# Two softmax additions ahead of a step's values and logits, and bank reads emitted with the last matmul

## The chip, the cores and the metric

The kernel runs on one core of a Trainium2 chip. The metric is the device time of one execution in microseconds (us). Three runs of the kernel before took 3520.87, 3521.09 and 3527.97 us; the median is 3521.09. Engines are named as in the profile: PE is TensorE (its weight loads are PEld), DVE is VectorE, ACT is ScalarE, POOL is GpSimd, SP is SyncE, which issues the DMAs.

## What is computed

Eight images of 512 channels and 32 x 32 pixels go through two layers, in float32. The reference, cut to what matters (`cbs` is a convolution, a batch norm and a SiLU; `_gn` is a group norm of 32 groups; `mask` lets only pairs of channels of one group through, `p` is a permutation):

```python
def bot_attention(x, qkv_w, rw, rh):          # x: 256 channels, 4 heads of 64
    q, k, v = conv2d(x, qkv_w, 0) ...
    logits = einsum('bhdi,bhdj->bhij', q, k + (rw + rh)) * 64 ** -0.5
    a = softmax(logits, axis=-1)              # 1024 x 1024 per head
    return einsum('bhij,bhdj->bhdi', a, v)

t = cbs(x, cv1_w, cv1_bn, 0)                  # on _gn(x)
ys = [t[:, :256], t[:, 256:]]
for i in range(2):
    z = cbs(ys[-1], m_cv1_w[i], m_cv1_bn[i], 1)           # 3x3
    z = bot_attention(z, m_qkv_w[i], m_rw[i], m_rh[i])
    z = silu(bn_eval(conv2d(z, m_cv2_w[i], 0), m_cv2_bn[i]))
    ys.append(ys[-1] + z)
x = x + cbs(concatenate(ys), cv2_w, cv2_bn, 0)            # layer 0
x = x + (1x1 conv of _gn(x) with conv * t_gain * mask * s_gain)[:, p[p]]   # layer 1
```

## The kernel before

**Softmax units.** The attention of one image and block is cut into four units: two pairs of heads (`hp`) by two halves of 512 query columns. With 8 images and 2 blocks these are 64 units. The logits are made transposed: 128 keys stand on the partitions, 512 queries in the free dimension, one PSUM bank for each head of the pair. A unit has eight pieces `t` of 128 keys (`KT`). `logits(t)` makes two banks `lg` on PE (L435), ACT copies each to an SBUF tile `st` (L441), and DVE takes the running maximum `mx` from the bank (L446, from t = 1 on). `top` transposes the maxima on PE (`mt`, L454) and reduces them on DVE (`nm`, L455); `spread` transposes them back, over all partitions, into the PSUM tile `mb` (L462). `soften(t)` adds `mb`, which holds the negated maximum, to `st` on DVE (L466), takes the exponential on ACT in place (L467) and adds up on POOL (`sum`, L472). `values(t)` multiplies with v on PE into the one bank `po` (L478). `finish` sums over the partitions on PE (`den`, L490), copies on ACT (`rb`, L492); `divide` takes the reciprocal and multiplies on DVE, in halves (L497, L499).

**Steps.** The main loop runs over 16 slots (image, block) of four units. A unit's four steps take t = 0, 2, 4, 6. A step treats two pieces of the unit `u`, two pieces of logits of the next unit `nxt`, and then a share of background work (`advance`). The maxima of `nxt` and the additions of `u` are tied in the order in which they are emitted (`in_turn`): on DVE none passes another. What else stands between them is set by the Tile scheduler, which orders each engine's instructions by when its own model has them ready.

**Background work.** `filler` goes through a slot's list (`slot_filler`): the 3x3 convolution of the next slot (`conv3`, by a transform in six products `m`), its projections (`project`: `qk`, `v`), the second 1x1 convolution of the slot before (`conv_m2`), and from a queue (`Background.take`) the first convolution of later images (`First`), the concatenated convolution (`Second`: `cv2`) and the second layer (`Last`: `l1`). Each is a generator that emits matmuls and yields a price in us; `advance` takes from it until the share of the step is reached. `accumulate` (L166 to L174) emits the matmuls of one sum into one bank and yields 1.72 after each two of them, the last time after the last matmul; only when it is resumed does the caller emit the reader of the bank (for instance `bn_silu`, L130 on ACT) and what follows it. `conv3` and `project` yield in the same way between the last matmul of a product and its readers. After product 4 these readers are six DVE operations, L288 to L293.

**Buffers.** One pool of five PSUM banks (`ps_f`) serves logits, `mt`, `den` and all background sums; `mb` has two banks and `po` one of their own. Which bank a new tile gets follows from the order in which the tiles before are released in the scheduler's model. The `st` tiles have ten buffers.

Of the kernel before, what the change touches and what calls it, by code (L numbers as in the profile page):

```python
# [22 lines left out]
P = 128  # L23
NB = 8
CT = 4
# [14 lines left out]
def conv_preact_kernel(ctx: ExitStack, tc: tile.TileContext, x, cv1, cv2, mcv1, qkv, mcv2, bn, rw, rh, conv, s_in, t_in, out):  # L40
# [92 lines left out]
    class GroupNorm:  # L133
# [30 lines left out]
        def apply(self, k, dst, src):  # L164
            nc.scalar.activation(dst, src, AF.Identity, bias=self.off[:, k : k + 1], scale=self.rstd[:, k : k + 1])  # L165


    def accumulate(ps, terms):

        for n, (w, moving) in enumerate(terms):  # L170
            nc.tensor.matmul(ps, w, moving, start=(n == 0), stop=(n == len(terms) - 1))  # L171
            if n % 2 and n < len(terms) - 1:
                yield 1.72
        yield 1.72 if len(terms) % 2 == 0 else 0.86  # L174

    class Image:
        def __init__(self, n):
# [23 lines left out]
        def conv1(self, h, tiles, order=(1, 0)):  # L201
            n = self.n
            for cp in order:
                w = weights(f"w_cv1_{n}_{h}_{cp}", (CT, 256), cv1[cp])
                for co in range(IT):
                    ps = bank(f"cv1_{n}_{cp}_{co}_{h}")
                    yield from accumulate(ps, [(w[:, k, ts(co, P)], tiles[k // 2][:, k % 2]) for k in range(CT)])
                    t = half_tile(f"y0_{n}_{cp}_{co}_{h}")
                    bn_silu(t, ps, BN_CV1 + IT * cp + co)
                    load(y_dram[n][cp][:, co, ts(h, HALF)], t)  # L210

        def load_y(self):
            assert self.halves == 2
# [4 lines left out]
        def conv3(self, i):  # L218
# [15 lines left out]
            def product(r, u):  # L234
                w = weights(f"w_m1_{name}_{r}", (IT, IT, 3, P), w_m1[i][r])
                ps = bank(f"m1_{name}_{r}")
                terms = [(c, dx) for c in range(IT) for dx in range(3)]
                for co in range(IT):
                    for j, (c, dx) in enumerate(terms):
                        nc.tensor.matmul(  # L240
                            ps[:, ts(co, 256)].rearrange("p (t x) -> p t x", x=F),
                            w[:, co, c, dx],
                            u[:, 9 * c : 9 * c + 8, dx : dx + F],
                            start=(j == 0),
                            stop=(j == len(terms) - 1),
                        )
                        if j % 3 == 2 and (co, j) != (1, 5):
                            yield 1.33
                yield 1.33
                self.ps = ps  # L250

            z = self.z = qp.tile([P, IT, HW], F32, tag="z", bufs=1, name=f"z_{name}")
# [20 lines left out]
            stt(inner(u4), b, -2.0, a, ALU.mult, ALU.add)  # L273
            yield from product(1, u1)
            nc.scalar.copy(mm[:, 0], self.ps)
            yield from product(2, u2)

            u0, u5 = plane(), plane()
# [3 lines left out]
            stt(inner(u5), b, -4.0, inner(u5), ALU.mult, ALU.add)  # L282
            nc.vector.tensor_tensor(ss[:, 0], mm[:, 0], self.ps, ALU.add)
            nc.vector.tensor_tensor(dd[:, 0], mm[:, 0], self.ps, ALU.subtract)
            yield from product(3, u3)
            nc.scalar.copy(mm[:, 1], self.ps)
            yield from product(4, u4)
            nc.vector.tensor_tensor(ss[:, 1], mm[:, 1], self.ps, ALU.add)  # L288
            nc.vector.tensor_tensor(dd[:, 1], mm[:, 1], self.ps, ALU.subtract)
# [1 line left out]
            stt(y[2], tx(ss[:, 1]), 4.0, tx(ss[:, 0]), ALU.mult, ALU.add)  # L291
            nc.vector.tensor_tensor(ss[:, 0], ss[:, 0], ss[:, 1], ALU.add)
            stt(dd[:, 0], dd[:, 1], 8.0, dd[:, 0], ALU.mult, ALU.add)  # L293
            yield from product(0, u0)
            nc.vector.tensor_tensor(y[0], tx(self.ps), tx(ss[:, 0]), ALU.add)
            yield from product(5, u5)
            nc.vector.tensor_tensor(y[3], tx(self.ps), tx(dd[:, 0]), ALU.add)
            for co in range(IT):
                bn_silu(z[:, co], z[:, co], BN_M1 + IT * i + co)


        def project(self, i):
            name = f"{self.n}_{i}"
            z = self.z
            self.q = qp.tile([P, IT, HW], F32, tag="q", name=f"q_{name}")
            self.k, self.v = [], []
            w = weights(f"w_qkv_{name}", (IT, 768), qkv[i])
            for hp in range(IT):
                k = kp_.tile([P, HW], F32, tag="k", name=f"k_{name}_{hp}")
                v = kp_.tile([P, KT, P], F32, tag="v", name=f"v_{name}_{hp}")  # L310
                self.k.append(k)
                self.v.append(v)
                load(k, r_dram[i][:, hp])
                for sel in (1, 0):
                    for h in range(2):
                        ps = bank(f"qk_{name}_{hp}_{sel}_{h}")
                        yield from accumulate(
                            ps, [(w[:, c, ts(IT * sel + hp, P)], z[:, c, ts(h, HALF)]) for c in range(IT)]
                        )
                        if sel == 0:  # L320
                            nc.scalar.mul(self.q[:, hp, ts(h, HALF)], ps, HD**-0.5)
                        else:
                            dst = k[:, ts(h, HALF)]
                            nc.vector.tensor_tensor(dst, ps, dst, ALU.add)
                for j4 in range(2):
                    ps = bank(f"v_{name}_{hp}_{j4}")
                    for j in range(4):
                        for c in range(IT):
                            nc.tensor.matmul(  # L329
                                ps[:, ts(j, P)],  # L330
                                z[:, c, ts(4 * j4 + j, P)],
                                w[:, c, 512 + P * hp : 512 + P * hp + P],
                                start=(c == 0),
                                stop=(c == IT - 1),
                            )
                    yield 1.77
                    nc.scalar.copy(v[:, 4 * j4 : 4 * j4 + 4].rearrange("p j c -> p (j c)"), ps)


        def conv_m2(self, i):  # L340
# [4 lines left out]
            for h in range(2):  # L345
                res = pair(gr, "gr", f"res_{name}_{h}")
                load(res, y_dram[n][1 + i][:, :, ts(h, HALF)])
                for co in range(IT):
                    ps = bank(f"m2_{name}_{co}_{h}")
                    yield from accumulate(ps, [(w[:, c, ts(co, P)], q[:, c, ts(h, HALF)]) for c in range(IT)])  # L350
                    t = half_tile(f"m2s_{name}_{co}_{h}")
                    bn_silu(t, ps, BN_M2 + IT * i + co)
                    dst = y_rows(co, h) if i == 0 else res[:, co]
                    nc.vector.tensor_tensor(dst, res[:, co], t, ALU.add)
                    load(y_dram[n][2 + i][:, co, ts(h, HALF)], dst)


        def load_ys(self, h):
# [7 lines left out]
        def conv2(self, h, ys):  # L366
# [3 lines left out]
            for cp in range(2):  # L370
                res = pair(gr, "gr", f"xr_{n}_{h}_{cp}")
                load(res, x[n, cp, :, :, ts(h, HALF)])
                for c in range(2):
                    co = 2 * cp + c
                    w = weights(f"w_cv2_{n}_{h}_{co}", (2 * CT, P), cv2[co])
                    ps = bank(f"cv2_{n}_{h}_{co}")
                    yield from accumulate(ps, [(w[:, k], ys[k // 2][:, k % 2]) for k in range(2 * CT)])
                    t = half_tile(f"cv2s_{n}_{h}_{co}")
                    bn_silu(t, ps, BN_CV2 + co)
                    nc.vector.tensor_tensor(res[:, c], res[:, c], t, ALU.add)  # L380
                    self.gn1.stats(co, h, res[:, c])
                load(x2_dram[n][:, h, 2 * cp : 2 * cp + 2], res)


        def load_x2(self, h):
# [12 lines left out]
        def last(self, h, xn):  # L398
            n = self.n
            for cp in range(2):  # L400
# [2 lines left out]
                w = weights(f"w_l1_{n}_{h}_{cp}", (CT, 256), w_l1[cp])  # L403
                for c in range(2):
                    ps = bank(f"l1_{n}_{h}_{2 * cp + c}")
                    yield from accumulate(ps, [(w[:, k, ts(c, P)], xn[k // 2][:, k % 2]) for k in range(CT)])
                    nc.vector.tensor_tensor(res[:, c], ps, res[:, c], ALU.add)
                load(out[n, cp, :, :, ts(h, HALF)], res)

    turn = []  # L410

# [329 lines left out]
    class Background:  # L741
# [15 lines left out]

        def take(self, us, force=False, wait=False):

            done = 0.0  # L760
            while done < us:
                if self.cur is None:
                    self.prepare()
                    if self.first == len(self.items):
# [2 lines left out]
                    if "setup" not in it.past or (clock.now < it.ready and not force):  # L767
                        if not wait:
                            return
                        done += 0.5  # L770
                        yield 0.5
                        continue
                    if clock.now < it.ready:
                        clock.flush()
# [3 lines left out]
                it, g = self.cur  # L778
                cost = next(g, None)
                if cost is None:  # L780
                    self.cur = None
                    continue
                done += cost
                yield cost
# [62 lines left out]
    def start_conv(im, tiles):  # L847
        n = im.n
        for cp in (1, 0):
            w = weights(f"w_cv1_{n}_{cp}", (CT, 256), cv1[cp])  # L850
            for h in range(2):
                for co in range(IT):
                    ps = bank(f"cv1_{n}_{cp}_{co}_{h}")
                    yield from accumulate(ps, [(w[:, k, ts(co, P)], tiles[h, k // 2][:, k % 2]) for k in range(CT)])
                    t = half_tile(f"y0_{n}_{cp}_{co}_{h}")
                    bn_silu(t, ps, BN_CV1 + IT * cp + co)
                    load(y_dram[n][cp][:, co, ts(h, HALF)], t)
        im.halves = 2

    first, second = images[:2]  # L860
# [22 lines left out]
    for s in range(len(slots)):  # L883
# [22 lines left out]
        for j in range(4):  # L906
# [9 lines left out]
            if before:  # L916
                before.finish()
                clock.tick(0.9)
            for t in range(0, KT, 2):
                if t:  # L920
                    u.values(t - 2)
                    u.values(t - 1)
                    clock.tick(2.0)
                u.soften(t)
                if before and t == 0:
                    before.divide(1)
                if nxt:
                    nxt.logits(t)
                    nxt.logits(t + 1)
                    clock.tick(2.0)  # L930
                u.soften(t + 1)
                advance((base + 4 + t) / steps)
            u.values(KT - 2)
            u.values(KT - 1)
# [62 lines left out]
```

## Time and profile before

| | |
|---|---|
| median of the three runs | 3521.09 us |
| the profiled execution, its own time | 3534.95 us |
| its span, first to last instruction | 3533.2 us |
| granted TensorE clock over the span | 0.974 |
| additions L466 | 512, 1212 ns each |
| exponentials L467 | 512, 1056 ns each |
| copies of logits L441 | 1024, 595 ns each |
| maxima L446 | 768 + 128, 680 and 677 ns each |
| sums on POOL L472 | 768 + 128, 1341 and 1328 ns each |
| table loads on ACT, before L130 and L467 | 130 and 128, 1283 ns each |

Times of instructions are of the one profiled execution. A wait row names who waited, for whom, the us in total, how often and the longest; the one named is the one that came last. A matmul of 512 columns in float32 stands as two records in the trace, some 0.43 us each at full clock, so that "x8" in a row of logits is four matmuls, of which those of two heads overlap. A timeline row has start, duration, engine, line, operation, output and inputs, a count, and in brackets the idle time of the engine before it and what ended it. The busy time of the matmuls grows when the clock is granted at half, so that a lower clock shows as PEclk and not as idle time.

### The profile page before, as it was taken

The page shows a single profiled execution, that of the slowest core. Times are in us where ns is not written, and L with a number is a line of the kernel's source. Part 1 is how long each engine was busy: PE and PEld are TensorE (multiplying, and loading weights), DVE is VectorE, ACT ScalarE, POOL GpSimd, SP SyncE. Part 2 cuts the span into 40 slices and gives each one's busy share as a digit, 9 for nine tenths or more (in the row PEclk, how much of TensorE's full clock was granted, in tenths as well). Part 3 has the DMA queues.
Part 4 walks back from the last instruction along what each step waited for, and adds up shares of the span by engine and source line. Part 5 has one row for each costly group of instructions (what it writes and reads, how often), then busy time and mean ns, then how long its engine had stood idle before and what let it go on. Part 6 is the DMA issues. An engine that isn't in the chain of part 4 may idle for free.

```text
span 3533.2 us, 33236 instructions
## 1 busy us (share of the span) xinstructions
PE 3306.7 (94%) x11716; PEld 1562.5 (44%) x11716; DVE 2113.4 (60%) x2717; ACT 1801.2 (51%) x2385; POOL 1257.0 (36%) x971
## 2 busy tenths in 40 slices
PE   6999998999999999999999999999999999999988
PEld 2645434343444445354444444354545344353333
DVE  4435555475756665576756665676756665666641
ACT  3045674755555544554555544645456544645631
POOL 2014333343433433343433334344434433334320
PEclk9899999999999999999999999999999999999989
DMA  7552352231223241333323141332323241523345
GB/s 276 204 199 88 98 173 75 90 107 45 102 75 116 66 143 66 103 130 100 109 80 116 60 152 63 131 113 96 101 94 103 68 148 53 165 67 107 114 160 173
DMA packets 142296, 400.35 MB, mean 113 GB/s; under 512 B 13104, under 2 KB 14384, under 8 KB 142128
## 3 DMA queue, kind: packets, MB, share of 16 engines
q1 hardware_dynamic: 141408, 397.99, 33.8%
q8 instruction: 93, 1.52, 0.2%
q14 instruction: 75, 0.61, 0.1%
q10 hardware_dynamic: 720, 0.23, 0.0%
HBM read 318.47 MB, written 79.69 MB: 113 GB/s over the span
## 4 chain that ended last, share of the span: by engine, by line
PE 62%; DVE 15%; ACT 9%; issue 7%; DMA 4%; POOL 3%; SPq 0%; ACTq 0%; POOLq 0%; DVEq 0%
PE cv L171 13%; PE m L240 9%; PE lg L435 9%; PE po L478 9%; PE l L171 5%; PE qk L171 5%; DVE mx L446 4%; DVE st L466 3%; PE v L329 3%; ACT st L467 3%; POOL sum L472 2%; DVE rb L497 2%; ACT st L441 2%; DMA x<-in_x 2%; PE den L490 2%
## 5 line engine op out<-in xcount | busy, mean ns | idle before, releaser
L472 POOL TENSOR_TENSOR sum<-sum,st 128x512 f32<-128x512 f32 x768 | 1009.3, 1341 | 833.4 <-ACT st L467 833.4
L467 ACT ACTIVATE st<-st 128x1024 f32<-128x1024 f32 x512 | 537.0, 1056 | 644.2 <-DVE st L466 636.9
L446 DVE TENSOR_TENSOR mx<-mx,lg 128x512 f32<-128x512 f32 x768 | 482.6, 680 | 499.2 <-ACT st L441 498.8
L441 ACT COPY st<-lg 128x512 f32<-128x512 f32 x1024 | 534.8, 595 | 328.5 <-PE lg L435 250.0
L466 DVE TENSOR_TENSOR st<-st,mb 128x1024 f32<-128x1024 f32 x512 | 609.8, 1212 | 74.2 <-PE mb L462 74.1
L435 PE MATMUL lg<-q,k 64*128 64x512 f32 x2048 | 620.7, 634 | 25.4 <-DVE mx L446 20.2
L478 PE MATMUL po<-st,v 128*64 128x512 f32 x2048 | 547.6, 622 | 61.1 <-ACT st L467 44.4
L240 PE MATMUL m<-plane,w_m 128*128 128x256 f32 x2304 | 540.7, 389 | 18.8 <-DVE mx L446 9.7
L472 POOL TENSOR_TENSOR sum<-st,st 128x512 f32<-128x512 f32 x128 | 167.2, 1328 | 969.0 <-ACT st L467 969.0
L240 PEld LDWEIGHTS m<-plane,w_m 128*128 128x128 f32 x2304 | 433.5, 193 | 152.9 <-issue 42.4
L171 PE MATMUL cv<-y,w_cv 128*128 128x512 f32 x1024 | 470.7, 603 | 9.0 <-DMA y<-y 6.8
L435 PEld LDWEIGHTS lg<-q,k 64*128 64x128 f32 x2048 | 211.9, 189 | 417.7 <-issue 280.4
L171 PEld LDWEIGHTS cv<-y,w_cv 128*128 128x128 f32 x1024 | 185.8, 191 | 257.7 <-issue 235.8
L478 PEld LDWEIGHTS po<-st,v 128*64 128x64 f32 x2048 | 115.6, 137 | 390.9 <-ACT st L467 169.3
L497 DVE RECIPROCAL rb<-rb 128x256 f32<-128x256 f32 x128 | 215.6, 1724 | 92.3 <-ACT rb L492 92.3
L171 PE MATMUL cv<-x,w_cv 128*128 128x512 f32 x512 | 243.3, 623 | 26.4 <-ACT x L165 15.3
L171 PE MATMUL qk<-z,w_qkv 128*128 128x512 f32 x512 | 234.0, 599 | 15.8 <-DVE mx L446 13.1
L171 PE MATMUL l<-x,w_l 128*128 128x512 f32 x512 | 236.2, 608 | 2.4 <-ACT x L165 2.4
L130 ACT ACT_TABLE_LOAD x130 | 166.8, 1283 | 17.7 <-PE m L171 14.5
L455 DVE TENSOR_REDUCE nm<-mt 128x4 f32<-128x512 f32 x128 | 82.3, 682 | 144.3 <-PE mt L454 144.3
L171 PEld LDWEIGHTS cv<-x,w_cv 128*128 128x128 f32 x512 | 97.1, 198 | 158.0 <-issue 113.2
L467 ACT ACT_TABLE_LOAD x128 | 164.2, 1283 | 2.2
(144 smaller groups left out, 2374.8 us busy)
## 6 DMA issues: line engine op xcount, KB each, us to landing
w_m<-w_m SPq DMA_DIRECT2D x96, 768.0 KB, 4.5
w_cv<-in_cv SPq DMA_DIRECT2D x92, 512.0 KB, 3.6
y<-y SPq DMA_DIRECT2D x64, 512.0 KB, 4.8
x<-in_x SPq DMA_DIRECT2D x56, 512.0 KB, 4.8
y<-y SPq DMA_DIRECT2D x64, 256.0 KB, 3.1
k<-r SPq DMA_DIRECT2D x32, 512.0 KB, 3.8
res<-y SPq DMA_DIRECT2D x32, 512.0 KB, 4.4
xr<-in_x SPq DMA_DIRECT2D x32, 512.0 KB, 4.2
```

Of the source, the lines that this page charges most:

```text
L130: nc.scalar.activation(dst, src, AF.Silu, bias=bn_b[:, col : col + 1], scale=bn_s[:, col : col + 1])
L171: nc.tensor.matmul(ps, w, moving, start=(n == 0), stop=(n == len(terms) - 1))
L240: nc.tensor.matmul(ps[:, ts(co, 256)].rearrange("p (t x) -> p t x", x=F), w[:, co, c, dx], u[:, 9 * c : 9 * c + 8, dx : dx + F], start=(j ...
L329: nc.tensor.matmul(ps[:, ts(j, P)], z[:, c, ts(4 * j4 + j, P)], w[:, c, 512 + P * hp : 512 + P * hp + P], start=(c == 0), stop=(c == IT - 1),)
L435: nc.tensor.matmul(lg[h], self.k[r, ts(t, P)], self.q[r, self.hp, ts(self.half, HALF)], start=True, stop=True)
L441: nc.scalar.copy(st[:, h], lg[h])
L446: in_turn(nc.vector.tensor_tensor(self.mx[:, h], so_far[:, h], lg[h], ALU.max))
L466: in_turn(nc.vector.tensor_tensor(st, st, flat(self.mb), ALU.add))
L467: nc.scalar.activation(st, st, AF.Exp)
L472: nc.gpsimd.tensor_tensor(self.acc[:, h], so_far[:, h], self.st[t][:, h], ALU.add)
L478: nc.tensor.matmul(self.po[HD * h : HD * h + HD], self.v[:, t, ts(h, HD)], self.st[t][:, h], start=(t == 0), stop=(t == KT - 1),)
L497: nc.vector.reciprocal(self.rb[:, r], self.rb[:, r])
```

## The change

Three things are changed. First, in a step both `soften(t)` and `soften(t + 1)` are emitted first, then the values of the step before, then the logits of the next unit; before, `soften(t)` stood between values and logits, and `soften(t + 1)` behind the logits. Second, a generator yields its last price after the reader of the bank and not before it; `accumulate` returns this price and the caller yields it. The price after the second half of a v bank is 0.89 and not 1.77. Third, the prices that close a sum are of the type `Whole`, and `take` ends only behind such a price, so that a task from the queue is not left in the middle of a sum when the list goes on to the next task. Where two sums share a store (`conv2`, `last`), the price of the second comes behind the store. The places not shown below change in the same way as those shown.

```diff
+    class Whole(float):
+        pass
     def accumulate(ps, terms):
         for n, (w, moving) in enumerate(terms):
             nc.tensor.matmul(ps, w, moving, start=(n == 0), stop=(n == len(terms) - 1))
             if n % 2 and n < len(terms) - 1:
                 yield 1.72
-        yield 1.72 if len(terms) % 2 == 0 else 0.86
+        return Whole(1.72)
...
-                    yield from accumulate(ps, [(w[:, k, ts(co, P)], tiles[k // 2][:, k % 2]) for k in range(CT)])
+                    us = yield from accumulate(ps, [(w[:, k, ts(co, P)], tiles[k // 2][:, k % 2]) for k in range(CT)])
                     t = half_tile(f"y0_{n}_{cp}_{co}_{h}")
                     bn_silu(t, ps, BN_CV1 + IT * cp + co)
                     load(y_dram[n][cp][:, co, ts(h, HALF)], t)
+                    yield us
...
-                yield 1.33
                 self.ps = ps
...
             yield from product(1, u1)
             nc.scalar.copy(mm[:, 0], self.ps)
+            yield 1.33
             yield from product(2, u2)
...
             yield from product(4, u4)
             nc.vector.tensor_tensor(ss[:, 1], mm[:, 1], self.ps, ALU.add)
             nc.vector.tensor_tensor(dd[:, 1], mm[:, 1], self.ps, ALU.subtract)
...
             nc.vector.tensor_tensor(ss[:, 0], ss[:, 0], ss[:, 1], ALU.add)
             stt(dd[:, 0], dd[:, 1], 8.0, dd[:, 0], ALU.mult, ALU.add)
+            yield 1.33
             yield from product(0, u0)
...
-                    yield 1.77
                     nc.scalar.copy(v[:, 4 * j4 : 4 * j4 + 4].rearrange("p j c -> p (j c)"), ps)
+                    yield 0.89
...
                     self.gn1.stats(co, h, res[:, c])
+                    if c == 0:
+                        yield us
                 load(x2_dram[n][:, h, 2 * cp : 2 * cp + 2], res)
+                yield us
...
         def take(self, us, force=False, wait=False):
-            done = 0.0
-            while done < us:
+            done, cost = 0.0, Whole()
+            while done < us or not isinstance(cost, Whole):
...
                         done += 0.5
-                        yield 0.5
+                        yield Whole(0.5)
                         continue
...
                 if cost is None:
-                    self.cur = None
+                    self.cur, cost = None, Whole()
                     continue
                 done += cost
                 yield cost
...
             for t in range(0, KT, 2):
+                u.soften(t)
+                if before and t == 0:
+                    before.divide(1)
+                u.soften(t + 1)
                 if t:
                     u.values(t - 2)
                     u.values(t - 1)
                     clock.tick(2.0)
-                u.soften(t)
-                if before and t == 0:
-                    before.divide(1)
                 if nxt:
                     nxt.logits(t)
                     nxt.logits(t + 1)
                     clock.tick(2.0)
-                u.soften(t + 1)
                 advance((base + 4 + t) / steps)
```

More of the change, by code (lines that the diff above doesn't have):

```diff
@@ L284, in conv3 @@
             nc.vector.tensor_tensor(dd[:, 0], mm[:, 0], self.ps, ALU.subtract)
+            yield 1.33
             yield from product(3, u3)
             nc.scalar.copy(mm[:, 1], self.ps)
+            yield 1.33
             yield from product(4, u4)
@@ L293, in conv3 @@
             stt(dd[:, 0], dd[:, 1], 8.0, dd[:, 0], ALU.mult, ALU.add)
+            yield 1.33
             yield from product(0, u0)
             nc.vector.tensor_tensor(y[0], tx(self.ps), tx(ss[:, 0]), ALU.add)
+            yield 1.33
             yield from product(5, u5)
@@ L299, in conv3 @@
                 bn_silu(z[:, co], z[:, co], BN_M1 + IT * i + co)
+            yield 1.33
         def project(self, i):
@@ L316, in project @@
                         ps = bank(f"qk_{name}_{hp}_{sel}_{h}")
-                        yield from accumulate(
+                        us = yield from accumulate(
                             ps, [(w[:, c, ts(IT * sel + hp, P)], z[:, c, ts(h, HALF)]) for c in range(IT)]
@@ L349, in conv_m2 @@
                     ps = bank(f"m2_{name}_{co}_{h}")
-                    yield from accumulate(ps, [(w[:, c, ts(co, P)], q[:, c, ts(h, HALF)]) for c in range(IT)])
+                    us = yield from accumulate(ps, [(w[:, c, ts(co, P)], q[:, c, ts(h, HALF)]) for c in range(IT)])
                     t = half_tile(f"m2s_{name}_{co}_{h}")
@@ L376, in conv2 @@
                     ps = bank(f"cv2_{n}_{h}_{co}")
-                    yield from accumulate(ps, [(w[:, k], ys[k // 2][:, k % 2]) for k in range(2 * CT)])
+                    us = yield from accumulate(ps, [(w[:, k], ys[k // 2][:, k % 2]) for k in range(2 * CT)])
                     t = half_tile(f"cv2s_{n}_{h}_{co}")
@@ L381, in conv2 @@
                     self.gn1.stats(co, h, res[:, c])
+                    if c == 0:
+                        yield us
                 load(x2_dram[n][:, h, 2 * cp : 2 * cp + 2], res)
+                yield us
         def load_x2(self, h):
@@ L405, in last @@
                     ps = bank(f"l1_{n}_{h}_{2 * cp + c}")
-                    yield from accumulate(ps, [(w[:, k, ts(c, P)], xn[k // 2][:, k % 2]) for k in range(CT)])
+                    us = yield from accumulate(ps, [(w[:, k, ts(c, P)], xn[k // 2][:, k % 2]) for k in range(CT)])
                     nc.vector.tensor_tensor(res[:, c], ps, res[:, c], ALU.add)
+                    if c == 0:
+                        yield us
                 load(out[n, cp, :, :, ts(h, HALF)], res)
+                yield us
     turn = []
@@ L853, in start_conv @@
                     ps = bank(f"cv1_{n}_{cp}_{co}_{h}")
-                    yield from accumulate(ps, [(w[:, k, ts(co, P)], tiles[h, k // 2][:, k % 2]) for k in range(CT)])
+                    us = yield from accumulate(ps, [(w[:, k, ts(co, P)], tiles[h, k // 2][:, k % 2]) for k in range(CT)])
                     t = half_tile(f"y0_{n}_{cp}_{co}_{h}")
@@ L857, in start_conv @@
                     load(y_dram[n][cp][:, co, ts(h, HALF)], t)
+                    yield us
         im.halves = 2
```

## The prediction

> **What bounds the kernel now.** I read the busy rows and the 40 slices first, then TensorE's waits, the granted clock by stretches, ScalarE's waits, and the timeline around one long wait. The first row says that TensorE works 94% of the span and no other engine more than 60%.
>
> ```profile
> PE 3306.7 (94%) x11716; PEld 1562.5 (44%) x11716; DVE 2113.4 (60%) x2717; ACT 1801.2 (51%) x2385; POOL 1257.0 (36%) x971
> ```
>
> So a gain can only come out of TensorE's idle time and out of its clock. The built order of both programs is, but for a few swaps, the same on TensorE up to the first unit's softmax (255 us) and from the last unit's maxima on (3360 us); what changes lies between. TensorE's waits in that stretch (who, on whom: us in total, times, longest):
>
> ```profile
> PE po L478 <- ACT st L467: 44.4, 44, 2.9
> PE lg L435 <- DVE mx L446: 20.2, 20, 1.9
> PE qk L171 <- DVE mx L446: 13.1, 19, 0.9
> PE po L478 <- DVE q L499: 10.0, 7, 2.5
> PE m L240 <- DVE mx L446: 9.7, 9, 3.2
> PE m L171 <- DVE mx L446: 8.3, 7, 1.9
> PE v L329 <- DVE mx L446: 8.2, 12, 0.9
> PE cv L171 <- DVE mx L446: 7.8, 8, 2.0
> ```
>
> All rows of that answer together make 156 us. Two kinds are most of it: values (po) that wait for an exponential, 44.4 us, and matmuls of any kind that wait for a maximum (mx), that is for a bank that its last reader has not left: 20.2 + 13.1 + 9.7 + 8.3 + 8.2 + 7.8 = 67.3 us. The other 44 us are spread over the division, activations and planes. The clock in the same stretch (us, busy times, then PEclk):
>
> ```profile
> 255.00:3360.00 3105.00, 2949.88 (x10726) 1384.81 (x10728) 1956.42 (x2448) 1693.64 (x2240) 1200.92 (x918) 0.98 0.31 101
> ```
>
> The records behind that 0.98 are stretches of half clock, 106 us in all, so about 53 us of work lost. They lie behind long waits; this is one (DVE, ACT and PE from 1555 us on):
>
> ```profile
> 1563.02 1.75 DVE L293 SCALAR_TENSOR_TENSOR dd<-dd 128x512 f32<-128x512 f32 x1
> 1564.69 1.87 DVE L446 TENSOR_TENSOR mx<-mx,lg 128x512 f32<-128x512 f32 x3
> ...
> 1567.12 0.67 DVE L446 TENSOR_TENSOR mx<-mx,lg 128x512 f32<-128x512 f32 x1
> 1567.72 2.34 DVE L466 TENSOR_TENSOR st<-st,mb 128x1024 f32<-128x1024 f32 x2
> ```
> ```profile
> 1560.07 2.05 ACT L441 COPY st<-lg 128x512 f32<-128x512 f32 x4 [1.17 <-PE lg L435]
> 1568.96 2.19 ACT L467 ACTIVATE st<-st 128x1024 f32<-128x1024 f32 x2 [6.84 <-DVE st L466]
> ```
> ```profile
> 1559.79 1.02 PE L435 MATMUL lg<-q,k 64*128 64x512 f32 x4
> ...
> 1570.07 1.08 PE L478 MATMUL po<-st,v 128*64 128x512 f32 x4 [2.87 <-ACT st L467]
> 1571.08 3.68 PE L435 MATMUL lg<-q,k 64*128 64x512 f32 x8
> ```
>
> The addition for the odd half of a step stands behind the four maxima of that step, these stand behind conv3's vector work (L288 to L293), the exponential behind the addition, and the values of the next step behind the exponential. TensorE waits 2.87 us, and then eight logit records take 3.68 us; elsewhere eight take 1.99. I matched the values' waits with the program by their order: 41 of the 44, 42.8 us, are for an odd half (t = 1, 3, 5, 7).
>
> **The additions moved ahead.** Nothing is added or removed: in each of 256 steps (64 units of four) one addition (1212 ns, L466), one exponential (1056 ns, L467) and two sums on GpSimd (1341 ns each, L472) move from behind the copies and maxima to ahead of them. No DMA moves with them. The values of an odd half no longer depend on the maxima of their own step: the 42.8 us go. I count 38 and leave 5 for units whose first steps come too soon behind the spread. Each exponential's sums start earlier too, and ScalarE's copies wait 74.2 us for sums (57 times), so that this wait can only shrink.
>
> What it may cost: a copy now stands behind two additions and two exponentials instead of one of each, 1.21 us on VectorE and 1.06 us on ScalarE, and behind the copies wait the maxima, and behind these the banks. The cover is ScalarE's idle time ahead of the copies:
>
> ```profile
> ACT st L441 <- PE lg L435: 245.6, 189, 4.1
> ACT st L441 <- POOL sum L472: 74.2, 57, 3.7
> ```
>
> 245.6 us over 256 steps is 0.96 us a step against 1.06. That alone would be thin. But the built order of the changed kernel puts the first addition directly behind the maxima of the step before in 172 of the 189 steps with t = 2, 4, 6, and both in 139, so they run in VectorE's idle time (40% of the span) while TensorE does background work. Bounds: nothing, and 67 x 1.06 us = 71 us if each of the 256 steps less the 189 idle ones pays a whole exponential. I take 10, near the lower end, because in 126 of 192 steps the built order has both exponentials side by side, and a late copy costs TensorE only when the 5.2 us of background sums (median of a step by the built order and 0.86 us a 512-column matmul) are over before the bank is free. A sentence of the Trainium skill speaks against this part: "TensorE: Matmul & The Clock Gate" (Architectural detail) has ScalarE and VectorE as strict FIFO, so a copy that is ready can't pass an exponential that isn't. The trace agrees (6.84 us of idle ScalarE at 1568.96).
>
> **Bank reads with the last matmul.** The generators now emit the readers before they hand back control. Readers, tables and stores stay as many; the stores go to SP's queue no later than before, and TensorE waits for no DMA in this stretch. The maxima waits fall in two kinds: 58 short ones (under 1 us, 36.1 us) and 17 long ones (31.4 us). The short ones are nearly all 0.6 us: the next background sum was given the bank of the step's first logits, 2.6 us behind their start, although the bank of the sum before had been read (a copy of v ends at 1406.99, the next v sum waits until 1410.77 for a maximum). The bank was given by the order of emission, and there the read came late. With it early, the older bank is free first. I take two thirds, 24 us; bounds 0 and 36. The long ones come where conv3's six operations (5.8 us) stand ahead of a unit's addition, so that exponential, copies and maxima all follow; five of 1.9 us are of this kind at the same place of the pattern. In the built order afterwards both additions stand ahead of those six operations in most of the sixteen convolutions, the maxima still behind. I take half, 16 us; bounds -15 (the maxima come later by as much) and 31. ScalarE's table loads fall from 260 to 244, 16 x 1283 ns = 20.5 us, beside TensorE's work: nothing.
>
> **Ends between sums, and the planner's prices.** The same matmuls run; a sum is no longer cut at a change of task, and two sums of v count 0.89 us instead of 1.77 while 16 records take 1.95. So steps with v get some 1 us more work for each and a later step 3.5 us less per projection. By the built order the thinnest step between logits 1 and values 0 grows from 0.2 to 3.6 us of background. I take nothing for it; bounds -10 and +10, the size of the division's waits (po <- q, 10.0).
>
> **The clock.** There are 28 waits of over 1.6 us (58.9 us together), and the half-clock stretches lie behind such waits. If half of them go, half of the 53 us does: 26 us; bounds 0 and 45. The same page of the Trainium skill (HAM oscillation) asks for gaps over about 3.4 us before the clock falls. By that rule waits of 2 to 3 us cost no clock and the sum would be 26 us smaller; the trace differs, as 3.68 against 1.99 us behind a wait of 2.87 shows.
>
> **Sum.** 38 + 24 + 16 + 26 - 10 = 94 us. The profiled execution took 3534.95 us (span 3533.2 and 1.7 around it), so 3441; the median of the runs is 3521.09, 14 us less, so 3427, and I say 3430.
>
> **Rivals.** (A) Only the odd exponentials gain, and the bank waits come back at other places, since five banks serve four logits and one sum as before: 38 us and a fifth of the clock's 53, less 10, about 39: 3482. For it: the long maxima waits are VectorE's own work. Against it: the short ones are an order of emission, which changes.
> (B) Slower: the copies are late by the second exponential. Place: the copy behind two exponentials, once per step. Price: the 71 us above and, as banks are then late by more than 1.6 us, another 40 of half clock, less 38 for the values and the clock behind them (10): 71 + 40 - 48 = +63, 3584. It decides as soon as more than some 45 of the 256 steps pay the exponential. For it: 0.96 against 1.06 us, and the FIFO. Against it: the additions' place in the built order.
> (C) Nothing: the planner's uneven steps and new waits for the row maxima (nm), now behind conv3's six operations in some units (3 or 4 times by the built order), eat it up: 3520. For it: the waits that are not po or mx, 44 us, are untouched.
> (D) Nearly all goes: 42.8 + 60 + 45 + 15 of the others, 163: 3358.
>
> **Chances.** Forecast 0.56, D 0.10, A 0.16, C 0.06, B 0.12. A measurement of this kernel tells 0.2%, 7 us, from no change. Faster 0.56 + 0.10 + 0.16 = 0.82, same 0.06, slower 0.12. The range takes in A and most of D and leaves B, C and the far end of D out: 3350 to 3515.
>
> **What would show it.** Right: po <- ACT st falls from 44 to under 8 us; the short mx waits to a third; PEclk in 255 to 3360 rises to 0.99; TensorE's idle time in that stretch falls from 156 to about 85 us. Wrong: ScalarE's idle time ahead of the copies is now VectorE's (ACT st L467 <- DVE st L466) while matmuls wait for mx more than 67 us (B); or mb <- nm becomes a row of more than 10 us (C).

## The result, and the profile after

| | before | after |
|---|---|---|
| median of four runs in turn | 3524.53 us | 3412.33 us (3409.66 to 3419.54) |
| ratio after to before, 95% interval | | 0.9674 [0.9655, 0.9692] |
| profiled execution, its own time | 3534.95 us | 3419.54 us |
| its span | 3533.2 us | 3417.8 us |
| granted clock over the span | 0.974 | 0.973 |

The change gains 112 us; 94 were forecast. The busy rows of the page of after, engine by engine, are as before: TensorE 94%, nothing else above 61%.

```profile
PE 3223.6 (94%) x11716; PEld 1559.5 (46%) x11716; DVE 2082.3 (61%) x2717; ACT 1759.5 (51%) x2369; POOL 1241.4 (36%) x971
```

TensorE's busy time fell by 83 us (3306.7 before) with the same number of instructions at the same clock. That was in no term of the sum. The costliest groups (busy us, mean ns of one, idle before and what ended most of it) show two rows that became cheaper, logits and values; first of before, then of after:

```profile
L435 PE MATMUL lg<-q,k 64*128 64x512 f32 x2048 | 620.7, 634 | 25.4 <-DVE mx L446 20.2
L478 PE MATMUL po<-st,v 128*64 128x512 f32 x2048 | 547.6, 622 | 61.1 <-ACT st L467 44.4
```
```profile
L453 PE MATMUL lg<-q,k 64*128 64x512 f32 x2048 | 555.1, 624 | 15.5 <-DVE dd L289 7.9
L496 PE MATMUL po<-st,v 128*64 128x512 f32 x2048 | 516.8, 618 | 31.4 <-ACT st L485 21.1
```

The mean of one record hardly moved, the sum did. 2048 logit records of 634 ns would be 1298 us, and the row has 620.7: what overlaps counts once, so the records of after overlap more. TensorE's waits from 255 to 3245 us, that is from the first softmax to just before the last logits, after (who, on whom: us in total, times, longest):

```profile
PE po L496 <- ACT st L485: 21.1, 14, 2.5
PE m L245 <- DVE z L303: 13.7, 6, 4.1
PE m L245 <- DVE mx L464: 12.8, 8, 3.6
PE l L175 <- DVE mx L464: 8.7, 3, 2.9
PE gm_a L146 <- DVE mv_a L144: 8.1, 4, 3.0
PE lg L453 <- DVE dd L289: 7.9, 3, 2.6
...
PE lg L453 <- DVE mx L464: 2.6, 4, 0.6
```

Values wait half as long, logits hardly for maxima any more; new are, among others, rows for `z` and `dd` (the vector work of conv3). The same stretch in one line: PEclk stands at 0.98, as before.

```profile
255.00:3245.00 2990.00, 2860.61 (x10714) 1381.24 (x10713) 1925.36 (x2450) 1649.35 (x2222) 1184.62 (x918) 0.98 0.32 105
```

To split the difference I gave TensorE's time from the first `mb` to the last one to the matmul that ran, from its start to the next start, less the wait ahead of the next, and kept apart half of the time at half clock (us, from the traces):

| kernel | waits | logits | values | all other matmuls | clock | span |
|---|---|---|---|---|---|---|
| before | 157.2 | 579.8 | 503.2 | 1823.0 | 48.6 | 3533.2 |
| after | 129.7 | 521.3 | 477.5 | 1818.2 | 53.9 | 3417.8 |

Waits give 27.5, logits 58.5, values 25.7, the rest 4.8; the clock takes 5.3. So 84 of the 111 us come from logits and values that take less time, though none was removed. The timeline shows how. A group here is a row of logits records on TensorE, or of values, with no other matmul between them; it is cut when another matmul is put inside. Before (start, us, work; wait in brackets):

```profile
1030.96 5.42 PE L171 MATMUL cv<-y,w_cv 128*128 128x512 f32 x12
1036.31 1.08 PE L478 MATMUL po<-st,v 128*64 128x512 f32 x4
1037.32 1.13 PE L435 MATMUL lg<-q,k 64*128 64x512 f32 x4
1038.37 1.08 PE L478 MATMUL po<-st,v 128*64 128x512 f32 x4
1039.38 1.13 PE L435 MATMUL lg<-q,k 64*128 64x512 f32 x4
...
1047.41 1.12 PE L435 MATMUL lg<-q,k 64*128 64x512 f32 x2
1048.46 1.08 PE L478 MATMUL po<-st,v 128*64 128x512 f32 x4
1049.47 1.98 PE L435 MATMUL lg<-q,k 64*128 64x512 f32 x6
```

And after:

```profile
1011.33 1.94 PE L496 MATMUL po<-st,v 128*64 128x512 f32 x8
1013.20 1.99 PE L453 MATMUL lg<-q,k 64*128 64x512 f32 x8
1015.12 5.42 PE L175 MATMUL cv<-y,w_cv 128*128 128x512 f32 x12
```

Eight records of logits together (four matmuls, two heads) take 1.92 us to the next start. Cut into two and six, the two take 1.05 and the six 1.91: six cost as much as eight, for the matmul whose partner of the other head is not beside it runs alone, and alone it takes as long as a pair (four records, 1.06). That cut costs 1.05 + 1.91 - 1.92 = 1.04 us. Cut in four and four it costs 2 x 1.06 - 1.92 = 0.20, and values in two halves 2 x 1.01 - 1.87 = 0.15. The odd exponentials were late before, and so, as the run with a free order on VectorE below bears out, the scheduler put odd values between the logits or behind some of them. Groups of logits in the built order, by records:

| records | 2 | 4 | 6 | 8 | more |
|---|---|---|---|---|---|
| before | 64 | 32 | 53 | 183 | 1 |
| after | 23 | 12 | 8 | 226 | 7 |

At the durations of the timeline rows, logits and values in the built order come to 1106.5 us before and 1033.5 after, 73 less. A wait inside a group cuts it too, on top of its own length: 12 groups of eight before and 5 after, 13.4 and 5.4 us beyond the waits.

"TensorEngine Tiling (Array Packing)" of the Trainium skill (Key Properties) says that tiles of the array run in parallel and that a change of tiling mode drains TensorE. Here logits use 64 rows, values 64 columns and the background all of the array; the 0.15 to 0.20 us of a cut that leaves pairs whole fits a drain, and the 1.04 us of a cut through a pair fits the lost parallel half.

### The profile page after: what moved, and what is told of

It is laid out like the page before. It is cut to its first block, busy times and chain, and to the rows that moved or that the text cites. A ratio compares the mean times of both kernels' runs of the same rounds, so it can differ in the third digit from the quotient of the medians.

```text
span 3417.8 us, 33275 instructions
## 1 busy us (share of the span) xinstructions
PE 3223.6 (94%) x11716; PEld 1559.5 (46%) x11716; DVE 2082.3 (61%) x2717; ACT 1759.5 (51%) x2369; POOL 1241.4 (36%) x971
## 4 chain that ended last, share of the span: by engine, by line
PE 63%; DVE 11%; ACT 6%; issue 6%; DMA 3%; POOL 2%; SPq 0%; POOLq 0%; DVEq 0%; ACTq 0%
PE cv L175 13%; PE po L496 10%; PE lg L453 10%; PE m L245 9%; PE qk L175 6%; PE l L175 5%; PE v L340 3%; DVE st L484 3%; ACT st L485 2%; PE den L508 2%; DVE mx L464 2%; PE mt L472 2%; DVE rb L515 1%; PE m L175 1%; PE mb L480 1%
## 5 line engine op out<-in xcount | busy, mean ns | idle before, releaser
L490 POOL TENSOR_TENSOR sum<-sum,st 128x512 f32<-128x512 f32 x768 | 998.4, 1330 | 710.1 <-ACT st L485 710.1
L245 PE MATMUL m<-plane,w_m 128*128 128x256 f32 x2304 | 543.6, 391 | 33.2 <-DVE z L303 13.7
L453 PE MATMUL lg<-q,k 64*128 64x512 f32 x2048 | 555.1, 624 | 15.5 <-DVE dd L289 7.9
L496 PE MATMUL po<-st,v 128*64 128x512 f32 x2048 | 516.8, 618 | 31.4 <-ACT st L485 21.1
L490 POOL TENSOR_TENSOR sum<-st,st 128x512 f32<-128x512 f32 x128 | 160.3, 1273 | 978.4 <-ACT st L485 802.4
L175 PE MATMUL cv<-y,w_cv 128*128 128x512 f32 x1024 | 463.5, 601 | 5.2 <-DMA y<-y 4.5
L453 PEld LDWEIGHTS lg<-q,k 64*128 64x128 f32 x2048 | 193.6, 187 | 370.1 <-issue 251.8
L496 PEld LDWEIGHTS po<-st,v 128*64 128x64 f32 x2048 | 125.0, 137 | 343.0 <-issue 220.2
L175 PE MATMUL l<-x,w_l 128*128 128x512 f32 x512 | 244.1, 625 | 19.7 <-ACT x L165 9.6
L175 PEld LDWEIGHTS l<-x,w_l 128*128 128x128 f32 x512 | 97.6, 199 | 147.4 <-issue 114.2
```

Source lines behind the costliest of these rows:

```text
L245: nc.tensor.matmul(ps[:, ts(co, 256)].rearrange("p (t x) -> p t x", x=F), w[:, co, c, dx], u[:, 9 * c : 9 * c + 8, dx : dx + F], start=(j ...
L453: nc.tensor.matmul(lg[h], self.k[r, ts(t, P)], self.q[r, self.hp, ts(self.half, HALF)], start=True, stop=True)
L490: nc.gpsimd.tensor_tensor(self.acc[:, h], so_far[:, h], self.st[t][:, h], ALU.add)
L496: nc.tensor.matmul(self.po[HD * h : HD * h + HD], self.v[:, t, ts(h, HD)], self.st[t][:, h], start=(t == 0), stop=(t == KT - 1),)
```

## The experiments

Two theories to start with. WAITS: the gain is that of the prediction, waits and what follows from them. RUNS: most of it is that logits and values stand in whole groups. Ratios are to before, run in turn on the same chip.

**Part one alone.** Before, with only the new step order:

```diff
+                u.soften(t)
+                if before and t == 0:
+                    before.divide(1)
+                u.soften(t + 1)
                 if t:
                     u.values(t - 2)
```

> Part one alone: both additions of a step first, bank reads and prices as before. Two theories. WAITS (the prediction's): the gain comes out of TensorE's waits, 38 us for the odd exponentials less 10, and no more, so 3524 - 28 = about 3495. RUNS (formed from the two traces): a group of four logit matmuls that stand together takes 1.99 us, a single one cut off 1.12 and the other three 1.98; two values together 1.08, four 1.94. By the built order logits and values take 1057 us at these prices against 1106 before, 49 less, and the po <- ACT st waits fall by some 23 us: about 3450.

3472.49 us, 0.9847 [0.9830, 0.9864]: 54 of the 112 us, between the two. The table's columns: waits 151.4, logits 548.1, values 494.7. Waits fall by 6 only, logits and values by 40. The values' wait for exponentials falls to 16.3 us, but 24 groups of logits now have a wait inside (26.4 us beyond it).

**Parts two and three alone.** After, with the old step order (the diff above, taken back).

> Parts two and three alone: bank reads with the last matmul, tasks end between sums, order of a step as before. WAITS: the bank waits' 40 us and a part of the clock, 50 us: about 3475. RUNS: by the built order logits and values take 1097 us against 1106, so 9 us less and what bank waits fall, 10 to 25: about 3500. By both the odd exponentials' waits (44 us) stay.

3488.50, 0.9889 [0.9874, 0.9903]: 39 us. Waits fall by 27 (157.2 to 130.1), the values' stay at 48.2. The two parts alone make 93 us, together 112.

**Part two alone.** The same, and the background may end within a sum again:

```diff
-            while done < us or not isinstance(cost, Whole):
+            while done < us:
```

> Part two alone: bank reads with the last matmul; order of a step and take's end as before. Together with reads_only (3488) it tells what ending between sums is worth under the old order; no_whole against the changed kernel gave 54 us under the new. If a task left in the middle of a sum holds a bank and so makes a logit matmul wait inside its group of four, lg <- mx stays near 19 us here (6.8 in reads_only, 18.7 in no_whole) and the time is about 3488 + 35 = 3520; logits and values by the built order 1112 us against 1097. If the early reads alone are the gain, 3490.

3517.01, 0.9966 [0.9950, 0.9983]: 8 us by the medians, 12 by the ratio; so some 27 to 31 of the 39 come with part three. Two wait rows of this kernel:

```profile
PE po L496 <- ACT st L485: 48.3, 47, 2.9
PE lg L453 <- DVE mx L464: 20.5, 19, 1.9
```

The logits wait for maxima 19 times, as before (20.2, 20 times); with part three it is 6.8 us, 4 times. The short waits for maxima (under 1 us) come to 37.5 us before, 30.0 with part two, 10.3 with parts two and three.

**Parts one and two.** After, with that same line put back.

> The changed kernel with part three taken out: take ends where its budget ends, in the middle of a sum or not. If ending between sums is worth something by itself, slower than 3412: by the built order logits and values take 1044 us against 1033, 11 us more: about 3423. If only the early reads count, 3412.

3465.89, 0.9812 [0.9787, 0.9838]: a miss for both numbers. Without part three 54 us of the 112 are gone (49 by the ratios), and the logits' waits for banks are back:

```profile
PE lg L453 <- DVE mx L464: 18.7, 19, 1.9
```

Its profiled execution was its fastest, 3453.41 us, and shows 35 us of this loss: waits 132.9, logits 543.4, values 487.7. Against after, 3 us of the 35 are waits and 32 are logits and values; 20 groups of eight have a wait inside (5 in after), which costs 21.8 us beyond the waits. That a task left within a sum holds a bank over the next logits follows from the code; shown is that these waits come and go with part three.

**Order tied, in before.** A manual order on PE keeps logits and values as they are emitted:

```diff
-                nc.tensor.matmul(
+                in_turn_pe(nc.tensor.matmul(
```

> The kernel before, with one thing added: logits and values are tied on TensorE in the order in which they are emitted, so that the scheduler can't put a values matmul between the four logits of a step. RUNS: by the built order logits and values take 1033 us against 1106, as in the changed kernel; 73 us less, less what new waits the tie makes for odd exponentials (up to some 40): 3450 to 3490. WAITS: a tie can only add waits; not faster than 3524, rather 10 us slower.

3554.86, 1.0082 [1.0065, 1.0100]. The groups got cheaper (logits 528.4, less 51), but (waits up to 3300 us):

```profile
PE po L484 <- ACT st L473: 97.2, 63, 3.9
PE lg L441 <- DVE mx L452: 31.3, 21, 4.9
```

The values wait over twice as long, and the clock costs 70.8 us and not 48.6. So whole groups gain nothing by themselves: a late exponential is paid either as cut groups or as waits. Whole groups are worth something only when their input is early.

**Order tied, in after.** The same edit on after.

> The changed kernel with the same tie. RUNS: logits and values 1015 us against 1033 by the built order, 18 us less: about 3394. WAITS: 3412 within its spread, or slower by new waits.

3415.26, 0.9682 [0.9665, 0.9699]: no gain. Logits 498.3, 23 less, but the first values of a unit now wait for the division (po <- q 32.8 us, 5.8 in after) that the scheduler had let other logits fill.

**Groups cut on purpose.** After, tied, with each group of logits cut once after its first matmul and the values apart:

```diff
+                    nxt.one(t, 0)
                     u.values(t - 2)
+                    nxt.one(t, 1)
+                    nxt.one(t + 1, 0)
+                    nxt.one(t + 1, 1)
+                    nxt.rest(t)
                     u.values(t - 1)
+                    nxt.rest(t + 1)
```

(`one` is a bank and its matmul, `rest` the copies and maxima.)

> The price of a cut group by itself: after_tied, with the order of a step made one logit matmul, two values, three logit matmuls, two values (t = 2, 4, 6); the same matmuls and no later inputs. By the built order 182 singles and 189 threes, logits and values 1254 us against 1015. RUNS, if the pieces' prices hold: 3415 + 239 = about 3650, with TensorE's idle time no higher than in after_tied (142 us). If a group's length is not a price of its own, 3415.

3526.92, 0.9997 [0.9982, 1.0012], 112 us more than tied after: all of the change's gain is gone, with the same matmuls and their groups cut. Logits take 691.9 us and values 499.8, 194 and 18 more; the expected time was too high mainly because waits fell to 74.0 (from 142.2) and the clock's cost to 29.2 (from 51.0). Its row of logits:

```profile
L461 PE MATMUL lg<-q,k 64*128 64x512 f32 x2048 | 737.1, 632 | 7.4 <-DVE dd L289 2.7
```

**Free order on VectorE, in before.** The tie between maxima and additions is left out:

```diff
-        if turn:
-            tc.add_manual_dep(instruction.ins, turn.pop().ins.name, IN_ORDER, reason="order of the softmax")
         turn.append(instruction)
```

> The kernel before without the tie between maxima and additions: emission as before, and the scheduler alone orders VectorE. It then puts the odd addition ahead of the maxima nearly everywhere. If the cause of both the waits and the cut groups is the odd addition's place behind the maxima, this is as fast as soften_only, about 3472 (logits and values by the built order 1037 us), and po <- ACT st falls under 20 us. If it is the place of the values in the emission, it stays near 3527. It can also be slower, where several additions run ahead and the maxima, and with them the banks, come later.

3453.48, 0.9780 [0.9760, 0.9802]: 75 us, more than part one. It confirms the cause that the prediction named, the odd addition held behind the maxima: with the scheduler free to pull it ahead, the values' wait is 14.8 us (44.4 before) and logits take 542.0.

**Free order, in after.**

> The changed kernel without the tie between maxima and additions. before_free (3453) was faster than soften_only (3472). If the tie itself costs, some 19 us less here too: about 3393. If the emission order already says what the scheduler would do, 3412 (logits and values by the built order 1037 us against 1033).

3415.79, 0.9694 [0.9679, 0.9709], as after: what the tie cost, part one has already taken.

**Tied, with logits first at t = 2.** The wait for the division is filled with the four logits:

```diff
+                if t == 2 and nxt:
+                    for j in range(4):
+                        nxt.one(t + j // 2, j % 2)
+                    u.values(t - 2)
+                    u.values(t - 1)
+                    nxt.rest(t)
+                    nxt.rest(t + 1)
```

> after_tied, with the logits ahead of the values at t = 2 only, where the values wait for the division of the unit before (po <- q, 32.8 us in after_tied against 5.8 in the changed kernel). If that wait is what ate the tie's 18 us, 3395 and po <- q under 10 us; if not, 3415.

3395.83 (3390.45 to 3405.09), 0.9623 [0.9599, 0.9647]: the fastest kernel of the study, 16 us below after. Three of its wait rows:

```profile
PE lg L461 <- DVE mx L475: 16.3, 13, 2.1
PE po L512 <- ACT st L501: 12.1, 12, 1.8
PE po L512 <- DVE q L533: 4.5, 1, 4.5
```

**The same in every step, and the same with VectorE free.**

```diff
-                if t == 2 and nxt:
+                if t and nxt:
```

> tied_t2 with the logits ahead of the values at t = 4 and 6 too. Groups are as whole as in tied_t2 (1012 us against 1016 by the built order), and values have 2 us more for their exponentials; but the copies of the logits wait for the values that still read their buffer, so the banks come 2 us later. If banks are what waits cost now, slower than 3396 by 20 to 60 us with matmul <- mx waits up; if the values' waits are, 3385.

> tied_t2 (3396) without the tie between maxima and additions. Free tie worth something: 3380. Not: 3396.

The first took 3416.74, 0.9696 [0.9681, 0.9710], 21 us more than with t = 2 alone. Logits ahead of the values ask for banks sooner, and waits for maxima grow (of other matmuls 52.5 us against 38.7, of logits 22.2 against 16.3). But waits for exponentials (1.4 against 12.1) and for `z` (0.5 against 8.6) shrink, so that all waits from the first `mb` to the last come to the same, 118.7 us against 118.1. The time stands in the logits themselves, 537.0 against 519.8, with 14 groups of eight that have a wait inside against 9 (19.0 us beyond the waits against 10.4), and in the clock, 44.6 against 35.7. The second took 3446.43, 0.9785 [0.9766, 0.9804], and was expected faster: free, VectorE does conv3's work at other times, and logits wait for its operations (lg <- dd 26.4 us, lg <- mx 22.6). So with PE's order fixed, leaving VectorE's order free cost 51 us here; why the scheduler's model chose so is open.

Part three alone, and parts one and three without the early reads, were not tried.

## Why the prediction was right or wrong

**Values, 38 us.** The mechanism held and the term was even short for it: by their order in the trace the waits of odd halves fell from 42.8 to 1.2 us. But the row fell only to 21.1, not under 8, because even halves wait now (19.8 us, 1.6 before), all of it in four units, one of each sixteen. This is one:

```profile
1588.91 1.08 PE L496 MATMUL po<-st,v 128*64 128x512 f32 x4 [1.95 <-ACT st L485]
1589.92 1.12 PE L453 MATMUL lg<-q,k 64*128 64x512 f32 x2
1590.97 1.08 PE L496 MATMUL po<-st,v 128*64 128x512 f32 x4
1591.98 1.98 PE L453 MATMUL lg<-q,k 64*128 64x512 f32 x6
1595.60 1.08 PE L496 MATMUL po<-st,v 128*64 128x512 f32 x4 [1.63 <-ACT st L485]
```

There is no background between its steps: from its first values to those of t = 6 TensorE spends 0.0 us on other matmuls than logits and values, in all four such units; before it was 0.0, 16.0, 16.0 and 16.0, and without part three 0.0, 16.1, 16.1 and 16.1. Without part three the latter three units have no such wait; with it they have 14.5 of the 19.8 us. So the uneven shares that the prediction put at nothing are real and cost part of this.

**Bank reads, 24 + 16 us.** The short waits fell by 27.7 (37.5 to 9.8), the long ones by 5.7 (35.4 to 29.7). The sum is near, 33 for 40. The reason for the short ones was half wrong: I gave them to the order in which reads are emitted, and part two alone takes 7.5 of them, part three with it 27.2. The 16 us for the long ones rested on a reading that holds for a part of them only. Five of them, waits of logits of 1.9 us each, stood behind conv3's six operations in the trace of before, and these five are gone. The others stood behind other work of VectorE (divisions, planes, additions to activations), and waits of that kind are there after the change as well; three new ones (9.8 us) stand behind the six operations, now by products of conv3 and not by logits. That the long ones are VectorE's own work the rival with 39 us had said.

**Ends between sums, 0 us (bounds -10 and 10).** This step failed: the ends between sums are worth some 27 to 31 us in the old order and 49 to 54 in the new.

**Cost, -10 us.** Late copies cost little: TensorE's waits for them grew from 2.3 to 8.8 us, while ScalarE's wait for logits is 191.6 us (245.6 before) and that for sums 32.1 (74.2). The 6.84 us of idle ScalarE that the prediction sets beside this term show no copy that was held back, since the next logits started only behind them, at 1571.08 us. More of the cost came elsewhere, in matmuls behind conv3's operations: `z` 13.7 and `dd` 7.9 us. One such wait, TensorE first and then VectorE:

```profile
1671.55 2.01 PE L453 MATMUL lg<-q,k 64*128 64x512 f32 x8
1677.64 8.49 PE L245 MATMUL m<-plane,w_m 128*128 128x256 f32 x24 [4.08 <-DVE z L303]
```
```profile
1669.92 2.47 DVE L464 TENSOR_TENSOR mx<-mx,lg 128x512 f32<-128x512 f32 x4
1672.31 2.34 DVE L484 TENSOR_TENSOR st<-st,mb 128x1024 f32<-128x1024 f32 x2
...
1676.91 0.68 DVE L303 TENSOR_TENSOR z<-m,ss 128x512 f32<-128x512 f32 x1
```

Four maxima, both additions and two operations on planes (left out) run ahead of the `z` that reads a product's bank, and the next product waits for it. I had named what waits behind a late copy, and not what of conv3 waits behind the two additions on VectorE.

**Clock, 26 us.** Failed: -5. Waits of over 1.6 us went from 28 (58.9 us) to 31 (81.1 us), and half-clock stretches from 17 (106 us) to 22 (116 us), each of the 22 behind a long wait. The waits that went were short ones (of all waits 164 became 106), while 16 of the 17 stretches of before lay behind waits of 1.7 us or more.

**What was missing.** The cut groups, 84 us. The trace of before showed them (groups of two, four and six beside groups of eight at 1.99), and the prediction used such a row only for the clock. So it is in good part luck that the time came out inside the range: waits and clock gave 22 us (27.5 - 5.3) where 94 were counted, and the groups, in no term, the rest. TensorE's idle time in the stretch fell to 130, not to 85.

**The rivals.** The slower one (late copies) is refuted by the rows above, and so is that nothing is gained. The first rival, 39 us, is not far from the 27.5 us of the waits' column, but not for its reason: the bank waits did not come back (all waits for maxima fell from 72.9 to 39.5 us); other waits did. That nearly all goes, 163 us, is refuted by the 130 us of idle time that are left.

## What to carry to other kernels

When a busy engine's input comes late, look at what the scheduler put in the gap: it may have filled the wait by breaking up work that is cheap only while it stands together, and the loss then stands as busy time and in no row of waits. So count such groups in the built order of both programs and price them whole and cut. And here clock would have come back only with the long waits: count those by themselves before a gain in clock is written into a sum.

## What the runs showed of the hardware

Two matmuls of 64 rows, one for each half of the partitions, overlap only while they are neighbours: four in a row take 1.92 us, three 1.91, two 1.06, one alone 1.05. A wait of TensorE inside such a row costs about 1.1 us beyond the wait (13.4 us in 12 groups before).

The 22 half-clock stretches of after follow waits of 1.94 to 4.08 us, 16 of them waits under 3 us, and last 3.4 us (14 times), 6.8 (7 times) and 20.5 (once). Here is the wait of 2.63 us for `dd` (timeline), and the windows line from it on, with PEclk at 0.79:

```profile
1304.22 1.33 PE L453 MATMUL lg<-q,k 64*128 64x512 f32 x2 [2.63 <-DVE dd L289]
1305.48 6.86 PE L245 MATMUL m<-plane,w_m 128*128 128x256 f32 x24
```
```profile
1304.00:1312.00 8.00, 7.78 (x26) 5.78 (x26) 4.81 (x7) 3.29 (x4) 2.75 (x3) 0.79 0.00 0
```

The same 24 records take 5.45 us at full clock (in the fastest kernel's timeline). "TensorE: Matmul & The Clock Gate" of the Trainium skill (HAM oscillation) asks for gaps over about 3.4 us; the traces show half clock behind shorter ones, though in multiples of that length.
